# Layer 0's gated product of channel tile 2: from VectorE to GpSimd

## The chip, the cores and the metric

The kernel runs on one core of a Trainium2 chip. The metric is the device time of one execution in microseconds; the time before is the median of three runs. The engines are named as in the profile: PE (TensorE matmul) and PEld (its weight load), DVE (VectorE), ACT (ScalarE), POOL (GpSimd), SP (SyncE, which here only issues DMAs).

## What is computed

The input `x` is 4 images of 64 channels, 256 x 256, in float32. Four layers follow one another, each of the form `x = x + layer(group_norm(x))`. Only layer 0 is touched by the change:

```python
x = einsum('bchw,oc->bohw', x, w_in)             # 64 -> 384 channels
xf = rfft2(8x8 patches of x) * fft_filter        # a spectral filter for each channel
x = irfft2(xf)
x = depthwise 3x3 convolution(x, w_dw)           # 384 channels, zero padding
x1, x2 = split(x, 2)                             # 192 gate and 192 value channels
x = gelu(x1) * x2
out = einsum('bchw,oc->bohw', x, w_out)          # 192 -> 64 channels
```

Layer 1 is a 3x3 convolution, layer 2 a 1x1 convolution whose input is chosen per pixel, layer 3 a Fourier layer.

## The kernel before

**Tiles.** Layer 0 works in strips of 8 rows, 32 to an image and 128 in all (`NS`). The 384 channels after expansion are put into three tiles of 128 partitions: tile 0 holds gate channels 0 to 127, tile 1 the value channels that belong to them, and tile 2 the last 64 gate channels in partitions 0 to 63 and the last 64 value channels in partitions 64 to 127.

**Stages of a strip.** `transpose_x` and `transform_x` take the normalized rows to the spectrum of 8x8 patches on PE. `expand` (L310 matmul `psu`, L313 DVE multiplication by the filter into `up`) makes the 384 channels; `invert` (L348 matmul `psy`, L355 ACT copy) brings them back into the row buffers `y`. For tiles 0 and 1 `depthwise` runs the nine taps of the convolution on PE as 32x32 diagonal matmuls (L374, `psd`); `gate_part` (L385, ACT gelu into `h`) and `value_part` (L391, DVE multiplication of `h` by the values in PSUM) finish them.

**Tile 2** has its nine taps as element-wise work in the buffer `v` (128 partitions x 8 rows x 256): `vector_tap` 0 is an ACT multiplication (L407), taps 1 to 8 are DVE `scalar_tensor_tensor` instructions (L409), which read the shifted rows of `y` and the sum so far in `v` and write `v`. In the next round `vector_gelu` (L417, ACT) takes the gelu of the gate half, partitions 0 to 63 of `v`, four rows at a time, and writes it to partitions 64 to 127 of the buffer `g`. `vector_gate` (L424) multiplies `g` by the value half, partitions 64 to 127 of `v`, and writes the product back to `v`: for rows 0 to 3 (`m` = 0) to partitions 0 to 63, for rows 4 to 7 (`m` = 1) to partitions 64 to 127. `g` has one buffer, `v` has two, so the strip before can be multiplied while the taps of the present one run.

**After that** `project_vector` (L436) and `project_tensor` (L448) accumulate the output of the strip on PE in PSUM (`pso`), the first from `v`, the second from `h`; `add_residual` (L462, DVE) adds `pso` to the residual rows `r`; `finish` takes the statistics of the sum for the next layer's norm (L470, DVE) and writes the rows out by two DMAs from POOL's queue (L472).

**Order.** Inside layer 0 the order of PE, DVE and ACT is the order of the program text (`manual_schedule` names these three engines). POOL and SP are not named there; their order is left to the framework's planner, and in the trace POOL follows the text: the memsets of the border columns of the three `y` buffers (`new_y`, L320), then the two output DMAs of the strip before. All waits are made by the framework from what is read and written. Four pairs of PSUM banks are taken in turn by all PE stages (`pair`), so that a stage waits for the one four turns earlier to be read out. In round `t` the taps of strip `t` alternate with the gelus and products of strip `t - 1`.

Of the kernel before, what the change touches and what calls it, by code (L numbers as in the profile page):

```python
# [105 lines left out]
class _Net:  # L106
# [69 lines left out]
    def _layer0(self, ctx, dst):  # L176
        tc, nc, a, B, H, W = self.tc, self.nc, self.a, self.B, self.H, self.W
# [13 lines left out]
        halves = [slice(0, C), slice(C, 128)]  # L191
# [54 lines left out]
        x0, xns, xT, xf, ups, yt, lt, vt, ht, rt, po, bst1, gt = ({} for _ in range(13))  # L246
# [172 lines left out]
        def vector_gate(t, m):  # L419

            if m in gt:
                g = gt.pop(m)
                r = slice(4 * m, 4 * m + g.shape[1])
                nc.vector.tensor_mul(vt[t][halves[m], r], g[halves[1]], vt[t][halves[1], r])  # L424

        def project_vector(t):

# [73 lines left out]
        with ordered:  # L501
# [20 lines left out]
            for t in range(NS + 2):  # L522
# [9 lines left out]
                normalize_x(t + 2)  # L532
                vector_taps(t, 1)
                vector_gate(t - 1, 0)
                vector_gelu(t - 1, 1)
                vector_taps(t, 2)
                vector_gate(t - 1, 1)
                vector_taps(t, 3, 4)
                if t <= NS:
# [417 lines left out]
```

## Time and profile before

| | |
|---|---|
| median of 3 runs | 9110.63 us (9108.54 to 9111.92) |
| the profiled execution, its own time | 9071.08 us |
| its span | 9069.3 us, mean PE clock 0.925 |
| PE / PEld busy in the span | 8455.9 us (93%) / 4936.7 us (54%) |
| DVE busy | 6687.3 us (74%) |
| ACT busy | 3539.6 us (39%) |
| POOL busy | 476.2 us (5%) |
| layer 0 in the trace | from the start to about 5138 us |
| products of L424 | 257, median 1.222 us, the last starts at 5133.0 us |
| taps of L409 with 2048 elements | median 2.352 us |

The span is what the profile covers. Busy times are sums over an engine's instructions; an engine that is busy for 93% need not be the one that everything waits for. A wait is put down to the instruction that released it last. Durations below are from this one profiled execution, which was 39.6 us shorter than the median of the runs.

### The profile page before, as it was taken

Reading aid. Unit: us, or ns where it says so; the run is one execution under the profiler, and the core shown is the slowest. Engines: PE = TensorE matmul, PEld = TensorE weight load, DVE = VectorE, ACT = ScalarE, POOL = GpSimd, SP = SyncE. Lnnn points to the kernel's source line nnn. Section 1 sums busy time; section 2 is a strip of 40 time slices with the busy share of each in tenths; the row PEclk is TensorE's granted clock in tenths of the full one; section 3 lists DMA queues with packets and bytes.
Section 4 is the critical chain, followed back from the end, with each engine's and each line's share of the span. In section 5 each row is a group of like instructions: output and inputs, shape, how many; then the busy total and the mean of one; then the engine's idle time right before and its main releaser. Section 6 shows DMA issues by size and latency. Waiting matters only on the chain.

```text
span 9069.3 us, 380207 instructions
## 1 busy us (share of the span) xinstructions
PE 8455.9 (93%) x180838; PEld 4936.7 (54%) x180838; DVE 6687.3 (74%) x6105; ACT 3539.6 (39%) x3993; POOL 476.2 (5%) x1168
## 2 busy tenths in 40 slices
PE   5999999999999999999999899998999999899986
PEld 3556556656566656556666433333333333399975
DVE  6888888888888988888888633337999999700034
ACT  2444444444444444444444311114555555400000
POOL 0000000000000000000000000000000000000001
PEclk9999999999999999999999999999999999955555
DMA  5222222222222222212221488885545454543469
GB/s 117 60 59 59 57 54 53 57 62 59 60 45 59 58 59 59 51 45 46 46 46 43 106 225 224 212 210 128 131 126 130 127 131 126 126 139 112 83 218 367
DMA packets 593939, 947.47 MB, mean 104 GB/s; under 512 B 34580, under 2 KB 461156, under 8 KB 576004
## 3 DMA queue, kind: packets, MB, share of 16 engines
q1 hardware_dynamic: 517508, 654.67, 29.7%
q0 software_dynamic: 74880, 268.47, 10.1%
q8 instruction: 1419, 23.25, 1.1%
q14 instruction: 132, 1.08, 0.0%
HBM read 654.58 MB, written 268.44 MB: 102 GB/s over the span
## 4 chain that ended last, share of the span: by engine, by line
PE 57%; DVE 24%; issue 10%; DMA 6%; ACT 2%; SPq 0%; POOL 0%; DVEq 0%; POOLq 0%; ACTq 0%
PE psd L374 16%; PE ps L641 11%; DVE v L409 8%; PE psy L348 8%; PE psu L310 6%; PE psa L832 5%; DVE q L732 4%; DVE v L424 3%; PE psm L875 2%; PE one L767 2%; PE div L752 2%; DMA x<-xr 2%; DVE up L313 1%; DVE s L778 1%; PE psF L297 1%
## 5 line engine op out<-in xcount | busy, mean ns | idle before, releaser
L374 PE MATMUL psd<-y,diag 32*32 32x512 f32 x73296 | 2558.8, 598 | 13.9 <-issue 12.6
L409 DVE SCALAR_TENSOR_TENSOR v<-y,sb_w_dw,v 128x2048 f32<-128x2048 f32 x1024 | 2392.6, 2337 | 56.4 <-ACT v L407 30.7
L374 PEld LDWEIGHTS psd<-y,diag 32*32 32x32 f32 x73296 | 1476.2, 103 | 1001.0 <-issue 468.0
L355 ACT COPY y<-psy 128x512 f32<-128x512 f32 x1536 | 912.9, 654 | 1639.8 <-PE psy L348 1639.8
L313 DVE TENSOR_TENSOR up<-psu,flt 128x768 f32<-128x768 f32 x1024 | 966.8, 955 | 471.4 <-PE psu L310 451.5
L348 PEld LDWEIGHTS psy<-sb_c_bdft,up 64*64 64x64 f32 x49152 | 869.4, 135 | 513.8 <-issue 327.2
L348 PE MATMUL psy<-sb_c_bdft,up 64*64 64x64 f32 x49152 | 918.7, 220 | 128.4 <-issue 85.8
L767 PE MATMUL one<-xn,wp 64*64 64x512 f32 x8192 | 1026.7, 591 | 0.0
L641 PE MATMUL ps<-xn,wk 64*64 64x512 f32 x9216 | 1002.4, 592 | 9.0 <-ACT xn L157 9.0
L310 PE MATMUL psu<-win,xf 64*64 64x384 f32 x8192 | 870.9, 491 | 14.0 <-issue 12.5
L157 ACT ACTIVATE xn<-x,nb,r 128x1024 f32<-128x1024 f32 (+3 forms) x272 | 487.6, 1796 | 1008.6 <-POOL xn L623 809.7
L641 PEld LDWEIGHTS ps<-xn,wk 64*64 64x64 f32 x9216 | 346.1, 133 | 657.2 <-issue 657.1
L767 PEld LDWEIGHTS one<-xn,wp 64*64 64x64 f32 x8192 | 357.1, 133 | 563.1 <-issue 542.3
L647 DVE TENSOR_TENSOR xr<-xr,ps 128x512 f32<-128x512 f32 x256 | 173.8, 679 | 657.1 <-PE ps L641 657.1
L733 ACT ACTIVATE q<-q 128x2313 f32<-128x2313 f32 (+2 forms) x256 | 527.1, 2089 | 321.1 <-DVE q L732 321.1
L732 DVE TENSOR_TENSOR q<-xn 128x2313 f32<-128x2313 f32 (+2 forms) x256 | 622.0, 2489 | 7.5 <-ACT xn L157 7.5
L752 PE MATMUL div<-q,ones 64*64 64x512 f32 x4096 | 584.4, 597 | 0.0
L832 PE MATMUL psa<-eh,x 128*128 128x64 f32 x2048 | 439.0, 421 | 19.9 <-DMA x<-x 19.9
L832 PEld LDWEIGHTS psa<-eh,x 128*128 128x128 f32 x2048 | 437.5, 333 | 20.6 <-issue 18.5
L417 ACT ACTIVATE g<-v 64x1024 f32<-64x1024 f32 x257 | 271.1, 1055 | 328.6 <-DVE v L424 303.3
L385 ACT ACTIVATE h<-psd 128x1024 f32<-128x1024 f32 x258 | 250.3, 1022 | 310.1 <-PE psd L374 309.8
L752 PEld LDWEIGHTS div<-q,ones 64*64 64x64 f32 x4096 | 189.4, 134 | 281.2 <-issue 278.9
(99 smaller groups left out, 7857.0 us busy)
## 6 DMA issues: line engine op xcount, KB each, us to landing
x<-x SPq DMA_DIRECT2D x240, 640.0 KB, 7.8
xr<-x SPq DMA_DIRECT2D x256, 512.0 KB, 6.6
x<-xr POOLq DMA_DIRECT2D x256, 512.0 KB, 8.0
x<-x SPq DMA_DIRECT2D x128, 1024.0 KB, 9.3
st<-in_x_dram SPq DMA_DIRECT2D x256, 256.0 KB, 4.0
x<-in_x_dram SPq DMA_DIRECT2D x256, 256.0 KB, 4.8
out_dram<-x POOLq DMA_DIRECT2D x64, 1024.0 KB, 9.3
r<-in_x_dram SPq DMA_DIRECT2D x248, 256.0 KB, 4.2
```

Of the source, the lines that this page charges most:

```text
L310: nc.tensor.matmul(ps[halves[n], s, 0:384], xf[t][halves[s], n, 4 * g + k], win[halves[s]], start=True, stop=True)
L313: nc.vector.tensor_mul(ups[t, g][:, :, k, :], ps[:, :, 0:384], flt.broadcast_to([128, 2, 384]))
L348: nc.tensor.matmul(ps[halves[c], n, s, :, k, :], up[halves[n], s, k, i * 128 + c * C : i * 128 + (c + 1) * C], bdft[halves[n]], start=True ...
L355: nc.scalar.copy(yt[t][i][:, 3:11, w0 : w0 + 64].rearrange("p r (k n w) -> p n r k w", k=4, n=2), ps[:, :, s])
L374: nc.tensor.matmul(d[q // 2][quarters[j], q % 2], diag[quarters[q], i, k, :], rows_in(t, i, quarters[q], j, dy)[:, :, dx : dx + W], start= ...
L409: nc.vector.scalar_tensor_tensor(v, s, wdw[:, 2, k : k + 1], v, ALU.mult, ALU.add)
L641: nc.tensor.matmul(ps[s][halves[j]], wk[halves[s], k, :], xn[halves[s], r : r + 2, dx : dx + W], start=(k == 0), stop=(k == 8),)
L732: nc.vector.tensor_sub(t, p0, p1)
L733: nc.scalar.activation(t, t, AF.Square)
L752: nc.tensor.matmul(div[s][halves[j]], ones[halves[s]], part[halves[s], r : r + 2, o : o + W], start=(k == 0), stop=(k == 4),)
L767: nc.tensor.matmul(one[s][halves[j]], wp[halves[s], m, :], xn[halves[s], r + dy : r + dy + 2, dx : dx + W], start=(m == 0), stop=(m == 7),)
L832: nc.tensor.matmul(ps[:, c, :], x[:, n, c, wc * 128 : (wc + 1) * 128], eh[:, n, :], start=(n == 0), stop=(n == NH - 1),)
```

## The change

In `vector_gate` the multiplication is issued on GpSimd. Its operands, its place in the program text and everything around it stay. The 257 products leave DVE's written order and go to POOL, whose order the planner sets. The waits change with it: the product, gelu 1 and `project_vector` now have POOL on one side of them.

```diff
@@ -421,7 +421,7 @@
             if m in gt:
                 g = gt.pop(m)
                 r = slice(4 * m, 4 * m + g.shape[1])
-                nc.vector.tensor_mul(vt[t][halves[m], r], g[halves[1]], vt[t][halves[1], r])
+                nc.gpsimd.tensor_mul(vt[t][halves[m], r], g[halves[1]], vt[t][halves[1], r])
```

## The prediction

> **What bounds the kernel now.** The change lies in layer 0, so I read that layer only. First the table of stages: one image of layer 0 (32 strips of eight rows).
>
> ```profile
> 1370.00:2610.00 1240.00, 1169.44 (x36854) 745.02 (x36856) 1086.78 (x899) 580.47 (x727) 59.49 (x171) 0.98 0.25 57
> ```
>
> The columns after the length are PE, PEld, DVE, ACT and POOL busy. PE has work in 94% of the time, DVE in 88%, POOL in 5%. An average like this cannot say which of the two ends each wait, so next the chain of work for one strip (start, length, what; the strip repeats every 37.85 us, as the first product of the next strip starts at 2052.88 after 2015.03).
>
> ```profile
> 2009.73 0.68 DVE up L313
> ...
> 2012.66 2.33 DVE v L409
> 2015.00 0.03 issue
> 2015.03 1.23 DVE v L424
> 2016.26 0.02 issue
> 2016.28 2.35 DVE v L409
> 2018.63 0.03 issue
> 2018.66 1.23 DVE v L424
> 2019.90 0.02 issue
> 2019.92 2.36 DVE v L409
> ...
> 2024.57 0.69 DVE r L462
> 2025.27 0.04 issue
> 2025.31 1.16 PE psy L348 x64
> ```
>
> For 15.6 us the chain stays on DVE: tap 1, product 0, tap 2, product 1, taps 3 and 4, then the residual add r, which frees the PSUM pair that PE's next inverse transform (psy) needs. The other 22 us of a strip are mostly PE. Both products stand on this chain. How tight is it? The timeline has PE's third depthwise block running from 2010.24 for 9.75 us, so to 2019.99, against 2019.88 for the end of product 1; and PE's work in front of psy ends at 2023.98 + 0.88 = 2024.86, against 2025.31 when r lets psy go. So PE could gain only 0.45 us here if DVE were early, but nearly every microsecond that DVE loses is lost by PE. The list of waits over the whole layer (200 to 5100 us; total, times, longest) agrees:
>
> ```profile
> ACT g L417 <- DVE v L424: 298.4, 126, 8.9
> ...
> PEld psy L348 <- DVE r L462: 93.7, 107, 1.3
> ...
> PE pso L436 <- DVE v L424: 63.9, 27, 3.2
> ...
> PE psy L348 <- DVE r L462: 28.0, 75, 0.6
> ```
>
> In 107 of some 126 strips the weights of psy wait for r. The first row is the single g buffer: the second gelu waits until the first product has read the first.
>
> **Prices.** The groups of instructions in layer 0, each shape apart; DVE from one answer, then POOL from another (count, busy us, mean ns, idle before):
>
> ```profile
> L409 DVE SCALAR_TENSOR_TENSOR v<-y,sb_w_dw,v 128x2048 f32<-128x2048 f32 x979 | 2299.8, 2349 | 52.1 <-ACT v L407 26.9
> ...
> L424 DVE TENSOR_TENSOR v<-g,v 64x1024 f32<-64x1024 f32 x252 | 307.9, 1222 | 7.9
> ```
>
> ```profile
> L322 POOL MEMSET y<- 128x768 f32 x9 | 6.7, 741 | 0.5
> L153 POOL TENSOR_TENSOR r<-gvs,mhalf 128x1 f32<-128x1 f32 x6 | 3.4, 566 | 46.8 <-DVE gvs L151 46.8
> L336 POOL MEMSET l<- 128x256 f32 x9 | 2.8, 312 | 0.3
> ```
>
> No row is a product of this size on POOL, so I bound it. Memsets: 512 more elements cost 741 - 312 = 429 ns, 0.84 ns each, with 312 - 256 x 0.84 = 97 ns fixed. At that pace 1024 elements cost 0.96 us, and a memset reads nothing, so I take this as the lower end. The Trainium skill, GPSIMD Engine Reference, section "3.1 Elementwise — side-by-side cycle accounting", gives a two-input add about 2.6 cycles an element at 1.2 GHz (4497 ns for 2048): 1024 x 2.6 / 1.2 = 2219 ns, plus some 60 fixed, is an estimate of 2.28 us. The upper end is 2219 + the 566 ns that POOL's one-element power takes, 2.79 us. I take 2.28 us: 1.06 us above DVE's 1.222.
>
> **What the skill says on the wait.** SBUF — State Buffer, section "Who interferes with whom": a DVE instruction with two SBUF inputs contends with a GpSimd instruction that reads SBUF, and the one that comes second blocks until the first is through. Each vector tap reads y and v, both in SBUF, and the product on POOL reads g and v. The trace of before cannot agree or disagree: POOL does only memsets, DMA issues and six tiny powers in this layer, and the memsets read nothing (130 ns for 22 elements, taps running or not). The other DVE work of the strip (up, h, r, bn_stats) has at most one SBUF tensor and should not collide.
>
> **The change part by part.**
> (1) Off DVE: 256 products of 1.222 us and one of 0.687, 313.5 us in all, 2.45 a strip.
> (2) Onto POOL: the same 257. POOL has 59.5 us of work in 1240, so it has room, and its queue is in the right order for them: the memsets of the next y end at 2005.26, before the first gelu is through at 2013.23; the two output DMAs behind the products start at 2026.15, since they wait for r anyway. I assume that the planner, which sets POOL's order, puts the products between these. Then no other queue is passed: SP's loads are untouched.
> (3) New waits. POOL waits for ACT's gelu, gelu 1 waits for POOL (g has one buffer), PE's project_vector waits for POOL. What queues behind gelu 1 on ACT are the gelus of h, which start at 2019.69 and need PE first: 1.4 us of cover for a gelu 1 that starts at 2017.3 and ends near 2018.4 (below). Behind project_vector on PE queues everything.
> (4) Moved: taps 2, 3, 4 and r could come forward by 1.22 to 2.45 us. Without the collision they do; with it they don't.
>
> Now one strip with the collision, the waiting side getting the port when the other ends. The gelu is through at 2013.23, tap 1 has run since 2012.66 and ends at 2015.00. Product 0: 2015.03 to 2017.31. Tap 2, blocked until then: 2017.34 to 2019.69. Gelu 1 ends at 2018.4 and product 1 waits for tap 2: 2019.72 to 2022.00. Tap 3: 2022.03, tap 4 ends near 2026.8, r starts at 2026.69 in place of 2024.57. Both exits are late by 2 x 1.06 = 2.12 us: project_vector at 2022.04 in place of 2019.92, and psy at 2027.43 in place of 2025.31, with PE idle for it. So although the products left DVE, DVE stands blocked for them, and each costs POOL's time instead of DVE's. The half of the strip that PE sets (2025 to 2047) cannot give this back. Sum: 256 x 1.06 + one half-size (estimate 1.17 - 0.69 = 0.48) = 272 us. The profiled execution of before took 9071.08 us (span 9069.3) and the median of the runs is 9110.63, 39.6 above it; 9071 + 272 = 9343 for a profile like that, 9383 for the median. Handing the port over may cost some tenths more; overlap of one instruction's start with the other's end may save as much: both left at nothing.
>
> With POOL's ends instead: 0.96 us gives -0.26 x 256 = -67 us, if the port is still handed over in turn; 2.79 gives +1.57 x 256 = +402. The 19 strips where psy did not wait for r absorb a little, at most some 10 us.
>
> **Rivals.**
> (A) No collision. Product 0 runs 2013.3 to 2015.6, gelu 1 to 2016.7, product 1 to 2019.0, under taps 1 to 3; DVE is done early, PE keeps its own pace. The gain is what PE waited: 28 + 64 us from the rows above and some 10 to 20 of later waits on DVE, about 100: 9010. For it: POOL is empty and even the slower product beats the old finish of 2019.88. Against: the page's rule fits exactly these two instructions. This is the other side; what decides is whether a tap and a product overlap in time.
> (B') Collision, but the port is shared finely or the product is near 1.7 us when it has the port: +0.5 x 256 = +128, range 9130 to 9280. For it: DVE's fixed part (2.35 us against 2.13 for 2048 elements at 0.96 GHz, an estimate with the clock of the page VectorE: DVE Perf Modes) leaves gaps.
> (D) DVE's next tap takes the port back once before POOL: product 0 after tap 2 (2017.4 to 2019.7), product 1 after tap 3 (2022.1 to 2024.4), project_vector 4.5 us late; psy follows the PE work of 4.94 us (2019.92 to 2024.86), at 2029.3: 4.0 x 128 = 512, 9620.
> (C) DVE always wins: product 0 only when tap 4 is through at 2022.1, to 2024.4; gelu 1 to 2025.5; product 1 to 2027.8; psy at 2032.8, 7.5 us late: 960 us, 10070. Taps follow each other within 30 ns, which speaks for D and C; a waiting request being served first speaks against.
> (E) The two sides cancel (a cheap product, part of the collision): within 0.2%.
>
> **How the numbers follow.** My forecast 0.56; B' 0.12; D 0.11; C 0.07; A 0.11; E 0.03. The forecast's own range is 9300 to 9470. Leaving out A and C, about 0.18, the 80% range goes from 9105 to 9680. Slower by over 0.2% (18 us, about what a measurement of this kernel can tell from no change): 0.56 + 0.12 + 0.11 + 0.07 = 0.86; same 0.03; faster 0.11.
>
> **What would show it.** If I am right: taps 2 and 3 lengthen or start late by about 2.3 us in each strip, taps 5 to 8 stay at 2.35; POOL's product is listed at 2.3 us or more (its wait inside or ahead); PE's wait of pso for v L424 appears in nearly all strips at about 2 us in place of 27 times; the period grows from 37.85 to about 40; the later layers do not move. What would make me wrong: taps at 2.35 us under a running product (A), a product that ends only after tap 3 or 4 (D, C), a product's real pace away from 2.3 us, or products put behind other work in POOL's queue.

## The result and the profile after

| | before | after |
|---|---|---|
| median of the runs | 9109.58 us (9103.15 to 9111.92, 4 runs) | 9222.99 us (9220.23 to 9236.39, 4 runs) |
| ratio after to before | | 1.0129, interval 1.0111 to 1.0146 |
| span of a profiled execution | 9069.3 us, in a second profile 9097.8 us | 9222.6 us |
| last product of L424 starts at | 5133.0 us, in the second profile 5159.6 us | 5283.6 us |

The change makes the kernel slower by 113 us; the forecast was 272 us. All of it lies in layer 0: from the last product to the end of the span it is 3939 us after and 3936 to 3938 us before.

The stage table for the same stretch as in the prediction, for the changed kernel (PE, PEld, DVE, ACT, POOL busy):

```profile
1370.00:2610.00 1240.00, 1150.73 (x35743) 725.13 (x35715) 1090.09 (x816) 559.25 (x700) 262.89 (x224) 0.98 0.25 56
```

DVE has fewer instructions than before (816 against 899) and is as busy as before (1090 us against 1087). The groups of the changed kernel between 200 and 5100 us, each shape apart, say why:

```profile
L409 DVE SCALAR_TENSOR_TENSOR v<-y,sb_w_dw,v 128x2048 f32<-128x2048 f32 x947 | 2645.4, 2793 | 44.2 <-ACT v L407 19.0
...
L424 POOL TENSOR_TENSOR v<-g,v 64x1024 f32<-64x1024 f32 x244 | 811.3, 3325 | 1131.0 <-ACT g L417 1088.7 <-DMA x<-in_x_dram 40.9 <-DMA st<-in_x_dram 1.2
```

The mean tap went from 2349 to 2793 ns. It is not all taps: over the whole layer, 222 of the 1000 taps of 2048 elements last about 4.34 us (median) and nearly all others keep 2.352. The chain of work of one strip of the changed kernel (start, length, what) shows which:

```profile
2024.76 2.26 DVE v L409
2027.02 0.02 issue
2027.04 4.36 DVE v L409
2031.40 0.03 issue
2031.43 4.35 DVE v L409
2035.78 0.03 issue
2035.81 0.06 DVE v L409
2035.87 2.21 issue
2038.08 0.69 DVE r L462
2038.77 0.04 issue
2038.81 1.16 PE psy L348 x64
```

The products are gone from the chain, and taps 2 and 3 have swallowed them. POOL's products of that strip (start, length):

```profile
2025.26 3.98 POOL L424 TENSOR_TENSOR v<-g,v 64x1024 f32<-64x1024 f32 x1 [9.08 <-ACT g L417]
2030.41 3.22 POOL L424 TENSOR_TENSOR v<-g,v 64x1024 f32<-64x1024 f32 x1 [1.17 <-ACT g L417]
```

Each is recorded from before the end of one tap until well into the next. In each of the 222 long taps exactly one product ends: 2.19 us after the tap's start and 2.15 us before its end (medians). From tap 1 to r the DVE now needs 13.41 us (2024.67 to 2038.08) where it needed 11.91 (2012.66 to 2024.57), so 1.50 us more. The waits of the changed kernel (total, times, longest, same stretch):

```profile
ACT g L417 <- POOL v L424: 291.9, 122, 3.1
...
PEld psy L348 <- DVE r L462: 154.3, 115, 5.9
PEld pso L436 <- POOL v L424: 131.2, 107, 2.5
...
PE psy L348 <- DVE r L462: 81.9, 109, 5.2
PE pso L436 <- POOL v L424: 79.9, 90, 2.0
```

PE's wait of project_vector for the product went from 27 strips to 90, and its wait for r from 28.0 to 81.9 us.

**Not all strips pay.** In each of the first three images four strips take the statistics of two input tiles, 12 in all, and there DVE waits for the second tile's load. One of them in the second profile of before, DVE alone:

```profile
385.67 1.28 DVE L203 BATCH_NORM_STATS2 bst<-st 128x6 f32<-128x512 f32 x2
392.27 1.29 DVE L203 BATCH_NORM_STATS2 bst<-st 128x6 f32<-128x512 f32 x2 [5.32 <-DMA st<-in_x_dram]
393.47 2.33 DVE L409 SCALAR_TENSOR_TENSOR v<-y,sb_w_dw,v 128x2048 f32<-128x2048 f32 x1
395.84 1.22 DVE L424 TENSOR_TENSOR v<-g,v 64x1024 f32<-64x1024 f32 x1
397.09 2.35 DVE L409 SCALAR_TENSOR_TENSOR v<-y,sb_w_dw,v 128x2048 f32<-128x2048 f32 x1
399.47 1.22 DVE L424 TENSOR_TENSOR v<-g,v 64x1024 f32<-64x1024 f32 x1
400.73 4.74 DVE L409 SCALAR_TENSOR_TENSOR v<-y,sb_w_dw,v 128x2048 f32<-128x2048 f32 x2
405.79 0.69 DVE L462 TENSOR_TENSOR r<-r,pso 128x512 f32<-128x512 f32 x1 [0.32 <-PE pso L448]
```

and the same strip of the changed kernel, first DVE, then POOL:

```profile
393.06 1.27 DVE L203 BATCH_NORM_STATS2 bst<-st 128x6 f32<-128x512 f32 x2
400.26 1.29 DVE L203 BATCH_NORM_STATS2 bst<-st 128x6 f32<-128x512 f32 x2 [5.93 <-DMA st<-in_x_dram]
401.46 9.50 DVE L409 SCALAR_TENSOR_TENSOR v<-y,sb_w_dw,v 128x2048 f32<-128x2048 f32 x4
410.88 1.28 DVE L462 TENSOR_TENSOR r<-r,pso 128x512 f32<-128x512 f32 x2
```

```profile
394.89 2.38 POOL L424 TENSOR_TENSOR v<-g,v 64x1024 f32<-64x1024 f32 x1 [8.15 <-ACT g L417]
398.43 2.37 POOL L424 TENSOR_TENSOR v<-g,v 64x1024 f32<-64x1024 f32 x1 [1.16 <-ACT g L417]
```

While DVE waits for the load, POOL gets both products done: no tap is running, so they take 2.38 us each, they block nothing, and the four taps then need 9.5 us. Before, the products stood behind the wait in DVE's queue. From tap 1 to r it is 9.42 us in place of 12.32.

I took the spacing of the strips from the starts of tap 0 on ACT (L407), in the second profile of before and that of after. The 97 ordinary strips go from 38.26 to 39.68 us on average, +1.42 each, +138 in sum; the 12 strips with two statistics tiles from 46.10 to 43.04, -37 in sum; the 15 intervals around the changes of image cost +26, and the first and the last three of the layer +1 together. That is 128.6 us; the spans differ by 124.8 and the medians by 113.

### The profile page after: what moved, and what is told of

Same layout as the page of the kernel before. It is cut to its first block, busy times and chain, and to the rows that moved or that the text cites. A ratio compares the mean times of both kernels' runs of the same rounds, so it can differ in the third digit from the quotient of the medians.

```text
span 9222.6 us, 379881 instructions
## 1 busy us (share of the span) xinstructions
PE 8528.5 (92%) x180838; PEld 4952.5 (54%) x180838; DVE 6832.5 (74%) x5848; ACT 3541.5 (38%) x3993; POOL 1329.2 (14%) x1425
## 3 DMA queue, kind: packets, MB, share of 16 engines
q14 instruction: 130, 1.06, 0.0%
## 4 chain that ended last, share of the span: by engine, by line
PE 53%; DVE 28%; issue 10%; DMA 6%; ACT 2%; POOL 1%; SPq 0%; DVEq 0%; POOLq 0%; ACTq 0%
PE psd L374 14%; DVE v L409 13%; PE ps L641 11%; PE psy L348 8%; PE psu L310 5%; PE psa L832 5%; DVE q L732 4%; PE psm L875 2%; PE one L767 2%; PE div L752 2%; DVE up L313 2%; PE psF L297 1%; DVE s L778 1%; DMA x<-xr 1%; DMA st<-in_x_dram 1%
## 5 line engine op out<-in xcount | busy, mean ns | idle before, releaser
L409 DVE SCALAR_TENSOR_TENSOR v<-y,sb_w_dw,v 128x2048 f32<-128x2048 f32 x1024 | 2833.2, 2767 | 56.1 <-ACT v L407 29.5
L424 POOL TENSOR_TENSOR v<-g,v 64x1024 f32<-64x1024 f32 x257 | 851.0, 3311 | 1205.5 <-ACT g L417 1151.8
```

The source lines that it names most:

```text
L409: nc.vector.scalar_tensor_tensor(v, s, wdw[:, 2, k : k + 1], v, ALU.mult, ALU.add)
L424: nc.gpsimd.tensor_mul(vt[t][halves[m], r], g[halves[1]], vt[t][halves[1], r])
```

## The experiments

Each is timed against the kernel before on the same chip, which moves by some 15 us from chip to chip (medians 9102 to 9118). Differences below are against that run's own before, unless a control is named.

**Does POOL's reading block the taps?**

```diff
-nc.gpsimd.tensor_mul(vt[t][halves[m], r], g[halves[1]], vt[t][halves[1], r])
+for _ in range(2):
+    nc.gpsimd.memset(vt[t][halves[m], r], 0.5)
```

> Each product on POOL is replaced by two memsets of the same 64 x 1024 elements (the multiplication is left out): POOL is busy for about 1.9 us per product, in the same place and with the same waits, and reads nothing. Port theory (a tap that reads two SBUF tensors and a POOL instruction that reads SBUF exclude each other): taps 2 and 3 go back from 4.36 to 2.35 us, r comes about 2.5 us earlier than before the change, and the kernel is faster than before, 9000 to 9050 us. Rival (any POOL work on SBUF, writes too, holds the taps up): taps 2 and 3 at about 4.2 us, 9180 to 9230 us. Rival (the added chain gelu, POOL, gelu, POOL, project_vector is what is late, the long taps only go with it): taps back at 2.35 but the time still above 9150 us.

Measured: 9000.37 us against 9113.77, ratio 0.9871 (0.9857 to 0.9886). The groups of this run, taps and memsets:

```profile
L409 DVE SCALAR_TENSOR_TENSOR v<-y,sb_w_dw,v 128x2048 f32<-128x2048 f32 x968 | 2274.2, 2349 | 46.4 <-ACT v L407 20.6
```

```profile
L425 POOL MEMSET v<- 64x1024 f32 x496 | 469.3, 946 | 815.5 <-ACT g L417 744.6 <-DVE v L409 49.8
```

POOL is busy 1.9 us for each former product, at the same place in the program text, and no tap is longer than before (at most 2.355 us). The waits are not all the same: nothing reads `g` here, so gelu 1 no longer waits for POOL, and 296 of the 514 memsets touch no tap. But 217 run wholly under taps, and the 145 taps with more than half a microsecond of memset beside them last 2.342 us (median). So it is the reading product that excludes the taps, not POOL's writing to SBUF. The rival of the added chain is not refuted by this run, which loosens that chain. Against it stand the half product below, where gelu 1 still waits for POOL (107 times) and the kernel is fast, and the changed kernel, where the 1.50 us that DVE needs more account for the 1.42 of a strip. This run is also roughly the price of rival A, the case without collision: 113 us under before.

**What does an element cost?**

```diff
-nc.gpsimd.tensor_mul(vt[t][halves[m], r], g[halves[1]], vt[t][halves[1], r])
+k = slice(r.start, r.start + g.shape[1] // 2)
+nc.gpsimd.tensor_mul(vt[t][halves[m], k], g[halves[1], 0 : g.shape[1] // 2], vt[t][halves[1], k])
```

> Each product on POOL does the first two of its four rows, 512 elements in place of 1024 (half of the multiplication of channel tile 2 is left out). Port theory with a price per element[...]: the product alone takes about 1.2 us, and the blocked taps go from 4.36 to about 3.25 us, so that DVE loses 0.9 us per product in place of the 1.22 us that the product cost it: 9000 to 9060 us. Rival (the hand-over of the port is most of the price): blocked taps at 3.8 us or more, 9130 us or more.

Measured: 9009.03 us against 9113.77, ratio 0.9883 (0.9869 to 0.9898). The blocked taps last 3.252 us (median of 220), 0.900 over a free one; with 1024 elements they last 4.339, 1.987 over. So 512 more elements block a tap for 1.087 us more, 2.12 ns each, close to the prediction's estimate of 2.17 ns (2.6 cycles at 1.2 GHz) from the Trainium skill (GPSIMD Engine Reference, "3.1 Elementwise — side-by-side cycle accounting"). Carried back to no element, the block is -0.19 us: the hand-over costs nothing and gives a little back. A blocked tap loses 1.99 us to a product that alone takes 2.38, and 0.90 to a half product that alone takes 1.28. Half of the product costs DVE less than the 1.22 us of the whole one did, which is why this run is fast.

**One product at a time.**

```diff
-nc.gpsimd.tensor_mul(vt[t][halves[m], r], g[halves[1]], vt[t][halves[1], r])
+e = nc.gpsimd if m == 0 else nc.vector
+e.tensor_mul(vt[t][halves[m], r], g[halves[1]], vt[t][halves[1], r])
```

The second of the two runs has `m == 1`.

> Only product 0 (rows 0 to 3) on POOL, product 1 on DVE. Port theory: one tap of a strip (tap 2) lasts 4.36 us, r comes 0.79 us later than before in the 114 or so ordinary strips and a little earlier in the 12 strips with two statistics tiles, since product 0 runs while DVE waits for the load: about 9185 us. Rival (only the product that releases project_vector counts): no change from before, 9100 to 9120 us.

> Only product 1 (rows 4 to 7) on POOL, product 0 on DVE. Port theory: one tap of a strip lasts 4.36 us, r comes 0.79 us later in all strips, as product 1 stays behind DVE's statistics through product 0: about 9205 us. Rival (only the product that releases project_vector counts): all of the change's cost, 9215 to 9230 us.

Measured: product 0 alone 9161.48 us, +48 (ratio 1.005, 1.0035 to 1.0065); product 1 alone 9181.01, +67 (1.0069, 1.0052 to 1.0086). In each, one tap of a strip is blocked: 109 taps at 4.347 and 124 at 4.334 us. Both were expected some 25 us higher, but the order and the kind are as the port theory says: each product pays for itself, and the sum, 115, is what both cost together (113). The strips with two statistics tiles part as expected: 45.3 us on average with product 0 on POOL, which runs during the wait, and 47.5 with product 1 on POOL, against 46.1 before.

**Was the profiled execution of before an ordinary one?** The kernel before, once more.

> The kernel before, once more, with a profile. The sum of the prediction was made against a profiled execution of 9071 us, 39 us under the median of the unprofiled ones. If that execution was an odd one, the new profile takes about 9110 us and its ordinary strips are some 0.3 us longer than the 38.2 us (median) of the first; then the change costs an ordinary strip about 1.2 us and not 1.5. If profiling itself shortens this kernel, the new profile is at 9070 us too.

Measured: 9102.06 us median, 9097.8 in the profile. So profiling does not shorten it; the first profile, 9069.3, caught an odd execution, with ordinary strips of 38.06 us in place of 38.26. What made it faster is open. Against the first profile the change would seem to cost 153 us, against the second 125.

**Are the 12 strips what hides a part of the cost?** The second statistics tile is taken in the middle of the next round, so that its load has time:

```diff
-def next_stats(t):
+def next_stats(t, late=False):
...
-    for k in range(min(j, n) * NJ // n, min(j + 1, n) * NJ // n):
+    ks = range(min(j, n) * NJ // n, min(j + 1, n) * NJ // n)
+    for k in ks[1:] if late else ks[:1]:
         input_stats(b + 1, k, bst0s[b + 1], p_st)
...
                 if t - 1 in rt:
                     finish(t - 1)
+                if t > 0:
+                    next_stats(t - 1, late=True)
```

> The kernel before; in the 12 strips that take statistics of two input tiles, the second is taken in the middle of the next round, so that DVE has no wait for its load. Theory: these strips go from about 46 us to about 39 to 40: 12 x 6.5 = 75 us less than before, about 9035 us. Rival (the load is late for another reason): no change, 9110 us.

> The same edit on the changed kernel. Theory (in the 12 strips with the wait the change gains about 3 us, since the products no longer stand behind it on DVE): here that gain is gone and the change costs more than with the wait, by 12 x (3 + 1.2) = 50 us: about 165 us above its own control without the change, so about 9200 us. Rival (those strips have no part in the size of the cost): 113 us above the control, about 9150 us.

Measured: without the change 9016.63 us, ratio 0.9906 (0.9891 to 0.992); with it 9202.69, ratio 1.0101 (1.0081 to 1.012). The 12 strips are 39.0 us in the one and 40.8 in the other. With the wait gone the change costs 186 us and not 113, nearer to the expected 165 than to the rival's 113: 1.48 us for each of 126 strips, the 1.50 that the chain shows. By these medians the wait for the statistics hid 73 us of the cost; the spacing of the 12 strips themselves gives 58 us (+21.5 in sum with the wait gone, -36.7 with it). One of the four runs behind 9202.69 took 9174.59, so the 186 is not known to better than some 20 us.

**POOL's product where DVE reads one SBUF tensor.** The gelus and products of a strip move right behind its own tap 8, beside h, up and bn_stats:

```diff
-vector_gelu(t - 1, 0)
 normalize_x(t + 2)
-vector_taps(t, 1)
-vector_gate(t - 1, 0)
-vector_gelu(t - 1, 1)
-vector_taps(t, 2)
-vector_gate(t - 1, 1)
-vector_taps(t, 3, 4)
+vector_taps(t, 1, 2, 3, 4)
...
     vector_taps(t, 8)
+    vector_gelu(t, 0)
+    vector_gate(t, 0)
     value_part(t, d)
 for k, i in enumerate((2, 0, 1, None)):
+    if k == 2 and t <= NS:
+        vector_gelu(t, 1)
+        vector_gate(t, 1)
```

> The changed kernel with the gelus and the products of a strip right behind its own tap 8, in place of between taps 1 to 3 of the next round: they then run while DVE does work that reads at most one SBUF tensor (h, up, bn_stats). Port theory: no tap is blocked (taps at 2.35 us), up, h and bn_stats keep their durations beside a running product of about 2.3 us, and POOL gives the gain that the change could not: 9000 to 9060 us. Rival (a product on POOL slows whatever DVE runs): h, up or bn_stats lengthen by about 2 us and the time is above 9150 us.

Measured: 9099.43 us, ratio 0.9999 (0.999 to 1.0008). The groups of this run:

```profile
L409 DVE SCALAR_TENSOR_TENSOR v<-y,sb_w_dw,v 128x2048 f32<-128x2048 f32 x973 | 2286.8, 2350 | 72.0 <-ACT v L407 44.4
...
L313 DVE TENSOR_TENSOR up<-psu,flt 128x768 f32<-128x768 f32 x996 | 941.4, 955 | 552.6 <-PE psu L310 541.5
...
L424 POOL TENSOR_TENSOR v<-g,v 64x1024 f32<-64x1024 f32 x248 | 589.8, 2378 | 335.6 <-ACT g L417 335.6
L391 DVE TENSOR_TENSOR h<-h,psd 128x1024 f32<-128x1024 f32 x248 | 290.9, 1214 | 3.8 <-PE psd L374 3.6
```

The collision is gone on both sides: the product takes 2378 ns, taps, up and h have the 2350, 955 and 1214 ns of before, and this beside running products: 469 up and 136 h have at least 0.2 us of a product beside them and last 0.95 and 1.21 us. That the number of inputs read from SBUF decides is taken over from the prediction; h and up also differ from a tap in the operation, and no run parts the two. The gain did not come, and the expected time was wrong. In place of PE, DVE now waits; the waits of this run and, below, of the second profile of before:

```profile
DVE r L462 <- PE pso L448: 152.6, 110, 4.3
```

```profile
DVE r L462 <- PE pso L448: 8.8, 11, 1.3
```

That row alone does not explain the missing gain: the run with memsets has 141.8 us of the same wait and is some 100 us faster. Against that run the time is lost in three places. Ordinary strips take 38.33 us in place of 37.90; the two gelus more on ACT among the copies of psy are a suspect, but this is not shown. The strips with two statistics tiles stay at 46.0 in place of 42.9, and DVE's wait for their load is 95.9 us in sum, against 60.4 there. The last three intervals of the layer take 103.2 us in place of 85.0 (87.6 before).

**What is left to win.** Three kernels on one chip: the last one with the later statistics; only product 0 early on POOL, product 1 on DVE between taps 1 and 2, with the later statistics; and the later statistics alone, again. The edit of the second, without the one for the statistics:

```diff
-nc.gpsimd.tensor_mul(vt[t][halves[m], r], g[halves[1]], vt[t][halves[1], r])
+e = (nc.gpsimd, nc.vector)[m]
+e.tensor_mul(vt[t][halves[m], r], g[halves[1]], vt[t][halves[1], r])
...
-vector_gelu(t - 1, 0)
+vector_gelu(t - 1, 1)
 normalize_x(t + 2)
 vector_taps(t, 1)
-vector_gate(t - 1, 0)
-vector_gelu(t - 1, 1)
-vector_taps(t, 2)
 vector_gate(t - 1, 1)
+vector_taps(t, 2)
...
     vector_taps(t, 8)
+    vector_gelu(t, 0)
+    vector_gate(t, 0)
     value_part(t, d)
```

> Both edits together: gelus and products on POOL right behind tap 8, and the second statistics tile taken in the middle of the next round. Theory (ordinary strips are bound by PE and the order of ACT there, so that taking products off DVE is worth little once nothing waits for the statistics): about the same as the later statistics alone, 9010 to 9045 us. Rival (freeing DVE of 2.45 us a strip is worth what it was worth in the run with memsets, 83 us below before on top of what the statistics give): 8950 us or less.

> Only product 0 on POOL, right behind tap 8; product 1 on DVE between taps 1 and 2 of the next round; later statistics. ACT has one gelu less among the copies of psy that PE waits for. Theory: no tap is blocked, DVE is freed of 1.22 us a strip, ordinary strips come near the 37.9 us of the run with memsets: 8975 to 9010 us. Rival (the early gelu costs PE as much as DVE gains): 9015 us or more.

> The kernel before with the later statistics alone, again, on the chip of the two runs beside it: 9017 us.

Measured: both early 9036.90 us (ratio 0.9912, 0.9898 to 0.9927); product 0 early 8973.58 (0.9843, 0.9827 to 0.9859); later statistics alone 9025.83 (0.9903, 0.9888 to 0.9918). So the early place is worth nothing for two products, and the kernel with one is 52 us faster than the later statistics alone: its ordinary strips take 37.91 us, as with the memsets (37.90), against 38.33 with the later statistics alone and 38.55 with both early. This kernel beats both kernels of the study, by 144 us the one before, of which the later statistics alone give 92. Its product on POOL lasts 2380 ns, and its taps 2349. It also moves gelus and product 1; the same order with product 0 on DVE was not run, so how much of the 52 us is POOL's is open.

## Why the prediction was wrong

**What bounds a strip: right.** Taps, products and r on DVE were the chain, with almost no slack at project_vector and at r. Where DVE reached r 1.50 us later after tap 1, ordinary strips grew by 1.42.

**Queue and order: right.** POOL has the two products between the memsets of y and the output DMAs; PE, ACT and SP have the instructions of before.

**The price of a product on POOL, 2.28 us: right.** Alone it takes 2.38, so it was 0.10 too low. (The cover for gelu 1, 2018.4 to 2019.69, is 1.3 us and not 1.4; nothing hung on it.)

**The collision, and who is served: right.** A tap and a reading POOL instruction exclude each other, the waiting side comes next, taps 2 and 3 are blocked and tap 4 is not. The blocked taps rule out rival A for the kernel as it stands; the run with memsets says that its price was near: 9010 forecast, 9000 measured. Rivals C and D, in which DVE takes the port back, fall with the chain. One of the named signs came smaller: PE's wait for the product stands in 90 strips, but at 0.9 us on average (79.9 over 90) and not about 2. Why was not traced.

**"Handing the port over may cost some tenths more; overlap ... may save as much: both left at nothing": the first step that failed.** It saves. I put one whole product, with its start and its end, between two whole taps; but by the records about 0.2 us of the product's start lies under the tap before (it ends 2.19 us after the blocked tap's start, and alone takes 2.38) and about 0.2 us of the tap's start lies under the product's end (2.15 us are left of 2.35). A blocked tap loses 1.99 us against the 2.28 + 0.03 of the working. Over 2 products in 126 strips that is 81 us less.

**"Sum: 256 x 1.06", one strip taken for all: the second step that failed.** I had the row that says that DVE's product held PE up 27 times, up to 3.2 us, and did not ask which strips these were. In the trace 24 of the 27 lie in the 12 strips with two statistics tiles, two in each. The answer of the profile from which that row came had another that counts these strips:

```profile
DVE bst L203 <- DMA st<-in_x_dram: 58.6, 12, 5.8
```

There the change gains 3.1 us in place of losing 1.48 (two blocks at their measured size): 54 us less. The pair with the later statistics shows it: 186 us there, where the first step alone leaves 272 - 81 = 191, and 113 here.

Together: 272 - 81 - 54 = 137 us, against 124.8 between the spans and 113 between the medians. The rest, 12 to 24 us, was not traced to a step. The measured time falls into the case B' of the prediction, but for other reasons than those given there: the port is not shared finely, and the product alone is not near 1.7 us.

## What to carry to other kernels

Taking work off a busy engine can cost time where the new engine locks the old one out: look for what the two read at the same time, and try the work beside other instructions (a product of 2.38 us left h and up as they were, and cost a tap 1.99 us in the other place). That alone need not bring a gain, as the run with both products moved shows. Where two instructions exclude each other, reckon with the time for each element (2.12 ns here) and not with the recorded length, which holds the wait (3.98 and 3.22 us in the strip shown). And before a strip's difference is multiplied by the number of strips, sort the strips: a few with another wait can turn the sign.

## What the runs showed of the hardware

- The loss of a tap to a POOL product grows by 2.12 ns for each element and is smaller than the product's own time: 1.99 us against 2.38, 0.90 for half the elements. The Trainium skill (SBUF — State Buffer, "SBUF: two separate sides") has the loser blocked until the other is through; by the records about 0.2 us of each lies beside the other.
- Between taps and products each waiting side came next: in each of the 222 blocked taps one product ended, and none lost more than 2.11 us, less than one product's time, although before the change a tap started within 0.04 us of the tap or product before it.
- A memset of 64 x 1024 on POOL wholly under running taps took 0.945 us (median of 217), as long as one with no tap beside it (0.947), and left the taps at 2.33 to 2.35 us.
- Beside a running product on POOL, h and up (one input from PSUM) kept their 1.21 and 0.95 us.
